# Linear attention and expert FFN in fp32 on one core: the last block's scores taken ahead of the preceding block's values, and a 22nd buffer of expert weights

## The chip, the cores and the metric

One Trainium2 chip, one core of it. The metric is the time on the device in microseconds (us), the median of three runs. All data is fp32.

## What is computed

The input `x` is (4, 128, 64, 64): four images, 128 channels, 4096 tokens each. Two layers follow each other.

```
x = x + conv_attention(group_norm(x))          # layer 0: softmax(e1^T e2) over 4096 x 4096 tokens
t = tokens(x)                                  # (4, 4096, 128)

# layer 1, attention with a scan: 8 heads, q_proj (8, 128), W_kv (2048, 128)
k, v = silu(layernorm(t) @ W_kv)               # per head 128 keys and 128 values
s = q_proj . k                                 # one score per token and head
m = cummax(s);  e = exp(s - m)
out = cumsum(e * v) / cumsum(e)                # along the tokens
t = t + mean over heads(out)

# layer 1, experts: 64 experts, each takes its 8 best tokens
p = softmax(layernorm(t) @ gate_w^T) over the tokens;   topv, topi = top_k(p^T, 8)
pooled = sum of the 8 tokens weighted by topv           # (4, 64, 128)
h = gelu(pooled @ weight1[e] + b1);  o = h @ weight2[e] + b2
t[topi] += o * topv
```

The cut leaves out the layer norm ahead of the gate's sum and the reshapes. The expert weights are 64 experts x 2 matrices of 128 x 512: 64 units of 512 KB, where a unit is one matrix of two experts.

## The kernel before

**Stages.** Layer 0 takes about the first 1460 us of the span. Attention with the scan runs in `loop()` (L1133) over `NB` = 32 blocks of 512 tokens, about 25 us each. Then come the gate's end and the pooling of the chosen tokens, the experts in 16 groups of four (`first`, `turn`, `second`, `gather`, L1362 to L1414), and the sums that go out.

**A block n of the loop.** `keys(n + 1)` makes the keys of the next block (L364, L365: TensorE, then a Silu on ScalarE for each of 8 heads). `weights(n)` turns the exponentials `es` (L902), copies them (L904), and builds `em` on GpSimd (L917). `weighted` multiplies `em` by the reciprocal sums `rb` (L926, VectorE). `values(n)` makes the values: eight matmuls `pv` of 128 x 512 (L938), each followed by a Silu on ScalarE (L942). `totals(n)` sums values per group of 64 tokens (L954), and VectorE adds these up in `before` (L964). `score(n + 1)` (L839) and `scan(n + 1)` follow, and `outputs(n)` (L974, L981) makes the result, which L986 adds to `t`.

**The scan.** `scan` is a chain over four engines: a copy of the scores in two halves (L851, VectorE), a running maximum (L856), the difference (L860), an Exp on ScalarE (L861), a copy into `es` on GpSimd (L866), and on VectorE a running sum (L871) and its reciprocal (L876). `spread` sends the reciprocals through DRAM so that they reach all partitions: `rd<-rr` (L884) and `rb<-rd` (L891), on the queue of SyncE.

**What sets the order.** TensorE's order is written out by hand (`manual_schedule`). A planner orders the other engines, by the data they wait for and by its estimates; the program then runs each engine's list as it stands. So the place of an Exp among the Silus of ScalarE, or of a copy among VectorE's products, is fixed when the program is built. The banks that `pk`, `pe`, `gtr`, `pv`, `pl` and `ltr` use are one pool of three (`l1kv`): a `pv` waits until the third tile before it has been read.

**The gate.** For each block, `gate_stats`, `gate_norm` (a Sqrt on ScalarE, L91, then `xg` at L96), `gate_turn` (L1023, L1025 into `xt2`) and `gate_logits` (L1031, L1035, and a maximum at L1038) run one or two blocks behind. `xg` and `xt2` are two tiles of 512 columns. ScalarE changes its function table at each change among Silu, Exp and Sqrt.

**The weights.** `load_units` (L1238) issues the 64 units on SyncE's queue, in the order in which they are used. There are `NW` = 21 places: 13 of the pool `fw`, 6 in `room` (which holds the keys and turned tokens during the loop), `wks` and `wvs` (the projections). All 21 are asked for right after the loop; each goes out once its place is free. After that `first` and `second` of each group ask for two more, which wait until the unit 21 places earlier has been used.

Of the kernel before, what the change touches and what calls it, by code (L numbers as in the profile page):

```python
# [8 lines left out]
F32 = mybir.dt.float32  # L9
# [4 lines left out]
P = 128  # L14
# [4 lines left out]
def conv_attn_hybrid_kernel(  # L19
# [23 lines left out]
    nc = tc.nc  # L43
    B, C, N = x.shape
# [6 lines left out]
    BLK = 512  # L51
    NBLK = N // BLK
    CPB = BLK // P
# [48 lines left out]
    wks = resid.tile([C, NH, C], F32, tag="wks", name="wks")  # L102
# [680 lines left out]
    GRP = BLK // H2  # L783
    EG = E // QG
    NB = B * NBLK
    NW = 21

    def layer1(pre, ready):

# [5 lines left out]
        with ExitStack() as kept, ExitStack() as l1:  # L795
# [39 lines left out]
            def score(n, ks):  # L835
                pss = ps_s.tile([P, BLK], F32, tag="s", name=f"{pre}ps_{n}")
                for h in range(NH):
                    g, r = h % QG, h // QG
                    nc.tensor.matmul(  # L839
                        pss[g * QW : (g + 1) * QW, :], qz[:, h, :], ks[h],  # L840
                        start=(r == 0), stop=(r == NR - 1),
                    )
                return pss
# [80 lines left out]
            def weighted(ems, rbs):  # L924
                for em, rb in zip(ems, rbs):
                    nc.vector.tensor_mul(em, em, rb.rearrange("p s h j -> p (s h) j"))  # L926
                return [em.rearrange("p (s h) j -> p s h j", s=2) for em in ems]
# [69 lines left out]
            rden = lgp.tile([P, B // 2], F32, tag="rden", name=f"{pre}rden")  # L997

            total = lgp.tile([P, C], F32, tag="total", name=f"{pre}total")
            gmv, grs, xgs, gate_xts, picks, eighth, cts, lefts = {}, {}, {}, {}, {}, {}, {}, {}  # L1000

            def gate_stats(n):
# [4 lines left out]
            def gate_norm(n, engine):  # L1007
                grs[n] = gp.tile([P, CPB], F32, tag="grs", name=f"{pre}grs_{n}", bufs=2)
                root = roots(grs[n], gmv[n])
                xgs[n] = gp.tile([P, CPB, C], F32, tag="xg", name=f"{pre}xg_{n}")  # L1010
                for c in range(CPB):
                    normalise(
                        engine, xgs[n][:, c, :], n * CPB + c, gmv[n][:, c, 0:1],
                        grs[n][:, c : c + 1],
                    )

                nc.gpsimd.tensor_copy(rs1[:, bass.ts(n, CPB)], grs[n])
                return root

            def gate_turn(n, ps):  # L1020
                ptr = ps.tile([P, CPB, P], F32, tag="kv", name=f"{pre}gtr_{n}")
                for c in range(CPB):
                    nc.tensor.transpose(ptr[:, c, :], xgs[n][:, c, :], ident)  # L1023
                gate_xts[n] = gp.tile([P, BLK], F32, tag="xt2", name=f"{pre}xt2_{n}")
                nc.scalar.copy(gate_xts[n], ptr.rearrange("p c x -> p (c x)"))  # L1025

            def gate_logits(n, ps):
# [105 lines left out]
            def loop():  # L1133
                if ready:
                    ks = keys(0, xt_of[0], range(NH // 2, NH), kss, ps_kv)
                else:
                    for n in range(2):
                        turned(n, tokens(n, xl_place), xt_of[n], ps_kv, pre)
                    keys(0, xt_of[0], range(NH), kss, ps_kv, pre)
                made = scan(0, score(0, kss))  # L1140
                rbs = spread(0, made[1])
                for n in range(NB):
                    more = n + 1 < NB
                    if more:
                        ks = keys(n + 1, xt_of[n + 1], range(NH // 2), kss, ps_kv, pre)
                    if n >= 1:
                        gate_stats(n - 1)
                    if not more:
                        gate_norm(n - 1, nc.vector)
                    if n + 2 < NB:  # L1150
                        xls = tokens(n + 2, xl_place)
                    if n == 0:

                        banks = [
                            ps.tile([P, 2, BLK], F32, tag=tag, name=f"{pre}pk_{tag}")[:, 0, :]
                            for ps, tag in ((ps_o, "o"), (ps_t, "t"))
                        ]
                        ks += keys(
                            n + 1, xt_of[n + 1], range(NH // 2, NH), kss, ps_kv, pre, banks
                        )  # L1160
                    es, rr, _ = made
                    ems = weights(n, es)
                    if n >= 2:
                        gate_turn(n - 2, ps_kv)
                    if more and n > 0:
                        ks += keys(n + 1, xt_of[n + 1], range(NH // 2, NH), kss, ps_kv, pre)
                    k0 = n - (B // 2 * NBLK + 2)
                    with ExitStack() as order:
                        if k0 == 0:
                            with tc.issue_after(made[2][1]):  # L1170
                                order.enter_context(tc.issue_after(select(0)))
                        if 0 <= k0 < NBLK:
                            left = gp.tile([P, BLK], F32, tag="left", name=f"{pre}left_0_{k0}")
                            marked = pick_mark(0, k0, left)
                            if marked is not None:
                                order.enter_context(tc.issue_after(marked))
                        if 1 <= k0 <= NBLK:
                            order.enter_context(tc.issue_after(pick_turn(0, k0 - 1, ps_kv)))
                        if k0 == NBLK:
                            divisors(0)  # L1180
                        aas = weighted(ems, rbs)
                    vs, last = values(n, xt_of[n])
                    if n >= 2:
                        best = gate_logits(n - 2, ps_kv)
                    if not more:
                        gate_turn(n - 1, ps_kv)
                    if 1 <= k0 <= NBLK:
                        pick_add(0, k0 - 1)
                    with tc.issue_after(last):
                        if n >= 1 and more:  # L1190
                            gate_norm(n - 1, nc.gpsimd)
                        if n == 0 and ready:
                            roots(rs1[:, bass.ts(B - 1, NCH)], mv1[:, bass.ts(B - 1, NCH), :])
                    if n + 2 < NB:
                        copied[n + 2] = turned(n + 2, xls, xt_of[n + 2], ps_kv, pre)
                    totals(n, vs)
                    if not more:
                        best()
                        best = gate_logits(n - 1, ps_kv)
                    if more:  # L1200
                        pss = score(n + 1, ks)
                        with ExitStack() as order:
                            if 0 <= k0 < NBLK:
                                with tc.issue_after(copied[n + 2]):
                                    exp = pick_exp(0, k0)
                                order.enter_context(tc.issue_after(exp))
                            made = scan(n + 1, pss)
                        rbs = spread(n + 1, made[1])
                        if 0 <= k0 < NBLK:
                            with tc.issue_after(made[2][1]):  # L1210
                                pick_keep(0, k0)
                    outputs(n, rr, aas, vs)
                    if n >= 2:
                        best()
# [3 lines left out]

            l1.close()
            pool = opener(l1, pre)  # L1220
            fwp = pool("fw", NW - 2 - ROOM)
            fo = pool("l2fo")
            fs = pool("l2fs", 2)
            ps_a = pool("l2a", 4, space=PSUM)
# [13 lines left out]
            def load_units(m):  # L1238
                for _ in range(m):
                    n = len(unit_weights)  # L1240
                    if n >= len(units):
                        return

                    if n % NW >= NW - 2:
                        w = wvs if n % NW == NW - 1 else wks.rearrange("d h e -> d (h e)")
                    elif n % NW >= NW - 2 - ROOM:
                        w = room[:, n % NW - (NW - 2 - ROOM), :]
                    else:
                        w = fwp.tile([P, FH + FC * C], F32, tag="fw", name=f"{pre}fw_{n}")
                    nc.sync.dma_start(out=w, in_=fw[units[n][0], units[n][1]])  # L1250
                    unit_weights[units[n]] = w
# [2 lines left out]
                w = unit_weights[layer, e // 2].rearrange("p (i x) -> p i x", i=2)[:, e % 2, :]  # L1254
                return w.rearrange("p (c o) -> p c o", c=FC) if layer else w

            load_units(NW)

            eos = fo.tile([P, B // 2, C], F32, tag="eo", name=f"{pre}eo")

# [29 lines left out]
            with tc.manual_schedule(engines={mybir.EngineType.PE}):  # L1290
# [25 lines left out]
                pool_tokens(0, total)  # L1316
                backs(2, nc.vector)
                best = gate_logits(NB - 1, ps_a)
                with tc.issue_after(copied[pre, NB - 1]):
                    backs(2, nc.scalar)  # L1320
                best()
# [233 lines left out]
```

## Time and profile before

| | us |
|---|---|
| median of 3 runs | 2386.18 (2384.77 to 2386.82) |
| the profiled execution | 2384.92 |
| its span | 2383.2 |
| what lies around the span | 1.7 |
| TensorE busy | 2340.1 (98%) |
| VectorE busy | 1494.8 (63%) |
| ScalarE busy | 1208.1 (51%) |
| GpSimd busy | 304.2 (13%) |

The stages around the change, in times of the timeline (us from the span's start):

| stretch | what |
|---|---|
| 2212.6 to 2237.0 | block 30: keys of 31, values of 30, scores of 31, outputs of 30 |
| 2237.0 to 2263.1 | block 31: scan of 31, values of 31, outputs of 31 |
| 2263.1 to 2289.9 | gate of the last block, choice of tokens, pooling |
| 2289.9 to 2353.2 | the 16 groups of experts |
| 2353.2 to 2383.2 | sums and output |

A busy TensorE is not a TensorE at its peak, since the ends of matmuls are modelled. In a line of the timeline the first number is the start, the second the time from the start of the first to the end of the last instruction of the group; the bracket tells how long the engine was idle ahead of it and what ended that. The page's chain of work that ended last is empty in this profile, so the path is read from the timelines and the waits.

### The profile page before, as it was taken

The numbers are of one execution on the slowest core, as the hardware profiler recorded it, in microseconds if no ns is written. First come the engines' busy times: TensorE is split into PE (matmuls) and PEld (weight loads), VectorE is DVE, ScalarE is ACT, GpSimd is POOL, SyncE is SP. The second block draws the span as 40 slices with busy tenths as digits, with TensorE's granted clock in tenths as the row PEclk, the third lists the DMA queues.
The fourth block names the chain that finished last, engine by engine and source line by source line (L and its number), as shares of the span: only waits on it lengthen the run. The fifth ranks groups of instructions, "written<-read, shape, count | busy, mean of one in ns | idle before, by whom it ended". The sixth has DMA issues, their size and how long they took to land.

```text
span 2383.2 us, 45629 instructions
## 1 busy us (share of the span) xinstructions
PE 2340.1 (98%) x19416; PEld 1554.0 (65%) x19416; DVE 1494.8 (63%) x2593; ACT 1208.1 (51%) x1639; POOL 304.2 (13%) x338
## 2 busy tenths in 40 slices
PE   7999999999999999999999999999999999999897
PEld 3567777677778677778777775555555555655554
DVE  6666666666656666655555556666666677776655
ACT  5444444444443444443443335666666666666541
POOL 0000000000000000000000002333343333333300
PEclk9999999999999999999999999999999999999999
DMA  3200110000100000020000000212112121112388
GB/s 83 75 23 19 41 39 1 17 13 23 49 25 1 23 7 23 18 52 1 1 1 1 1 1 19 55 38 55 38 38 55 38 54 39 38 38 55 118 307 322
DMA packets 61765, 109.93 MB, mean 46 GB/s; under 512 B 10096, under 2 KB 35184, under 8 KB 61552
## 3 DMA queue, kind: packets, MB, share of 16 engines
q1 hardware_dynamic: 57824, 101.22, 14.8%
q10 hardware_dynamic: 3728, 5.71, 0.7%
q8 instruction: 154, 2.52, 0.4%
q14 instruction: 59, 0.48, 0.1%
HBM read 85.40 MB, written 8.91 MB: 40 GB/s over the span
## 4 chain that ended last, share of the span: by engine, by line


## 5 line engine op out<-in xcount | busy, mean ns | idle before, releaser
L608 PE MATMUL av<-pr,am 64*128 64x512 f32 x4096 | 1057.2, 591 | 0.0
L587 ACT ACTIVATE pr<-sc 128x1024 f32<-128x1024 f32 x512 | 523.8, 1023 | 675.4 <-PE sc L583 606.7
L590 DVE TENSOR_TENSOR acc<-acc,pr 128x1024 f32<-128x1024 f32 x480 | 587.0, 1223 | 436.0 <-ACT pr L587 435.9
L608 PEld LDWEIGHTS av<-pr,am 64*128 64x128 f32 x4096 | 634.6, 187 | 260.4 <-issue 45.2
L583 PE MATMUL sc<-e,e 64*128 64x512 f32 x2048 | 618.9, 594 | 1.9 <-DMA e<-ee 1.9
L583 PEld LDWEIGHTS sc<-e,e 64*128 64x128 f32 x2048 | 317.3, 188 | 106.5 <-issue 19.5
L364 PE MATMUL pk<-room,wks 128*128 128x512 f32 x508 | 238.3, 607 | 2.0 <-ACT room L365 1.7
L938 PE MATMUL pv<-wvs,room 128*128 128x512 f32 x512 | 227.0, 596 | 2.5 <-ACT v L942 2.1
L942 ACT ACTIVATE v<-pv 128x512 f32<-128x512 f32 x256 | 152.7, 597 | 69.7 <-PE pv L938 69.7
L938 PEld LDWEIGHTS pv<-wvs,room 128*128 128x128 f32 x512 | 97.0, 191 | 121.9 <-issue 114.2
L926 DVE TENSOR_TENSOR em<-em,rb 128x1024 f32<-128x1024 f32 x64 | 78.4, 1224 | 154.4 <-DMA rb<-rd 154.4
L828 POOL MEMSET ew<- 128x1024 f32 x1 | 1.0, 952 | 1360.9 <-PE av L608 1360.9
L365 ACT ACTIVATE room<-pk 128x512 f32<-128x512 f32 x254 | 146.8, 597 | 54.4 <-PE pk L364 54.2
L364 PEld LDWEIGHTS pk<-room,wks 128*128 128x128 f32 x508 | 89.4, 189 | 107.6 <-issue 79.0
L917 POOL TENSOR_TENSOR em<-et,mask 128x1024 f32<-128x1024 f32 x64 | 122.6, 1937 | 79.0 <-ACT et L904 79.0
L96 POOL TENSOR_SCALAR xg<-t,gmv,grs 128x128 f32<-128x128 f32 x120 | 95.2, 806 | 287.3 <-DVE grs L92 209.4
L974 PEld LDWEIGHTS po<-v,em 64*64 64x64 f32 x4096 | 111.6, 133 | 29.1 <-DVE before L964 26.7
L974 PE MATMUL po<-v,em 64*64 64x128 f32 x4096 | 119.9, 271 | 1.9 <-issue 1.9
L876 DVE RECIPROCAL rr<-rr 128x512 f32<-128x512 f32 x32 | 107.3, 3353 | 1.1
L861 ACT ACT_TABLE_LOAD x24 | 30.8, 1283 | 121.1 <-DVE ss L860 121.1
L964 DVE TENSOR_TENSOR before<-before,pt 128x128 f32<-128x128 f32 x256 | 72.6, 284 | 9.6 <-PE pt L954 3.8
L871 DVE TENSOR_TENSOR_SCAN rr<-ones,state,ss 128x512 f32<-128x512 f32 x28 | 42.0, 1501 | 48.7 <-ACT ss L861 46.6
(203 smaller groups left out, 2031.5 us busy)
## 6 DMA issues: line engine op xcount, KB each, us to landing
rb<-rd SPq DMA_DIRECT2D x128, 256.0 KB
fw<-in_fw_dram SPq DMA_DIRECT2D x40, 512.0 KB
room<-in_fw_dram SPq DMA_DIRECT2D x18, 512.0 KB
t<-in_xtok_dram SPq DMA_DIRECT2D x32, 256.0 KB
e<-ee SPq DMA_DIRECT2D x63, 128.0 KB
x<-in_x_dram SPq DMA_DIRECT2D x12, 512.0 KB
e<-ee SPq DMA_DIRECT2D x63, 64.0 KB
out_dram<-t SPq DMA_DIRECT2D x8, 256.0 KB
```

Of the source, the lines that this page charges most:

```text
L96: i = engine.tensor_scalar(out=dst, in0=t[:, chunk, :], scalar1=mean, scalar2=rs, op0=ALU.subtract, op1=ALU.mult)
L364: nc.tensor.matmul(pk, wks[:, h, :], xt, start=True, stop=True)
L365: nc.scalar.activation(kss[h], pk, AF.Silu)
L583: nc.tensor.matmul(sc[:, u, :], e2[halves[u], p, :], e1[halves[u], :], start=True, stop=True)
L587: nc.scalar.activation(pr, sc, AF.Exp)
L590: added.append(nc.vector.tensor_add(acc, acc, pr).ins)
L608: nc.tensor.matmul(av, am[h, j, :], pr[h, u, :], start=(j == 0), stop=(j == NCH - 1))
L876: inverse = nc.vector.reciprocal(rr, rr).ins
L917: nc.gpsimd.tensor_tensor(em, eq.unsqueeze(2).to_broadcast([P, 2 * NH, H2]), mask.unsqueeze(1).to_broadcast([P, 2 * NH, H2]), ALU.mult,)
L938: nc.tensor.matmul(pv.rearrange("p h d -> p (h d)"), xt[:, bass.ts(2 * q + s, P)], wvs[:, bass.ts(m, BLK)], start=True, stop=True,)
L942: last = nc.scalar.activation(v[:, bass.ts(m, HPB), :], pv, AF.Silu).ins
L974: nc.tensor.matmul(po[s * H2 : (s + 1) * H2, u, q, :], aas[q][half, s, h, :], vs[2 * q + s][half, h, :], start=(q == 0 and h == 0), stop=F ...
```

## The change

For block 30 alone (`n + 2 == NB`), `score`, `scan` and `spread` of block 31 are written ahead of `values(30)` instead of after `totals(30)`. In block 31, `gate_norm(30)` is written after `weights(31)` and `gate_turn(29)` instead of ahead of them. `xg` and `xt2` become the halves of one tile, `gate_room`. That tile is the 22nd place for weights: 21 units are asked for after the loop as before, and the 22nd after the last `gate_logits`, whose matmul is the last reader of the tile. The pool `fw` stays at 13 buffers.

```diff
-    NW = 21
+    NW = 22
...
+            gate_room = gp.tile([P, 2 * BLK], F32, tag="gate_room", name=f"{pre}gate_room")
...
-                xgs[n] = gp.tile([P, CPB, C], F32, tag="xg", name=f"{pre}xg_{n}")
+                xgs[n] = gate_room[:, :BLK].rearrange("p (c d) -> p c d", c=CPB)
...
-                gate_xts[n] = gp.tile([P, BLK], F32, tag="xt2", name=f"{pre}xt2_{n}")
+                gate_xts[n] = gate_room[:, BLK:]
...
-                    if not more:
-                        gate_norm(n - 1, nc.vector)
...
                     if n >= 2:
                         gate_turn(n - 2, ps_kv)
+                    if not more:
+                        gate_norm(n - 1, nc.vector)
...
                         aas = weighted(ems, rbs)
+
+                    sooner = n + 2 == NB
+                    if sooner:
+                        rr_next = scan(n + 1, score(n + 1, ks))
+                        rbs_next = spread(n + 1, rr_next[1])
                     vs, last = values(n, xt_of[n])
...
-                    if more:
+                    if sooner:
+                        made, rbs = rr_next, rbs_next
+                    elif more:
                         pss = score(n + 1, ks)
...
-            fwp = pool("fw", NW - 2 - ROOM)
+            fwp = pool("fw", NW - 3 - ROOM)
...
-                    if n % NW >= NW - 2:
-                        w = wvs if n % NW == NW - 1 else wks.rearrange("d h e -> d (h e)")
-                    elif n % NW >= NW - 2 - ROOM:
-                        w = room[:, n % NW - (NW - 2 - ROOM), :]
+                    part = n % NW - (NW - 3 - ROOM)
+                    if part >= 0:
+                        w = (
+                            *(room[:, i, :] for i in range(ROOM)),
+                            wks.rearrange("d h e -> d (h e)"), wvs, gate_room,
+                        )[part]
...
-            load_units(NW)
+            load_units(NW - 1)
...
                 best = gate_logits(NB - 1, ps_a)
+                load_units(1)
```

## The prediction

> **What bounds the kernel now.** The page's chain is empty, so I read, in order: the waits of TensorE from 2205 to 2266 us, the timelines of the engines there, the windows of 2 us for clock and DMA, then the experts' timeline. TensorE stands still in block 31 alone:
>
> ```profile
> PE pe L902 <- POOL es L866: 2.6, 2, 1.8
> PE pv L938 <- ACT v L942: 2.1, 1, 2.1
> PE po L974 <- issue: 1.9, 1, 1.9
> ```
>
> The columns are total, times, longest. The first row is the wait for the scan of block 31, since no keys of a block 32 cover it. TensorE:
>
> ```profile
> 2235.93 1.09 PE L981 MATMUL po<-before,rr 128*64 128x128 f32 x16
> 2238.80 0.44 PE L902 MATMUL pe<-ident,es 128*128 128x128 f32 x2 [1.77 <-POOL es L866]
> ...
> 2240.78 5.29 PE L938 MATMUL pv<-wvs,room 128*128 128x512 f32 x8
> 2248.17 3.70 PE L938 MATMUL pv<-wvs,room 128*128 128x512 f32 x8 [2.10 <-ACT v L942]
> ```
>
> Eight rows are four `pv`, which take 3.43 us where nothing stops them (7.03 us for sixteen rows, pitch 0.857 us per `pv`). Here the fifth starts 7.39 us after the first: 3.96 us are lost to ScalarE, which changes tables for a Sqrt between the first and the second Silu. VectorE in block 30, then ScalarE:
>
> ```profile
> 2225.77 1.22 DVE L926 TENSOR_TENSOR em<-em,rb 128x1024 f32<-128x1024 f32 x1 [4.66 <-DMA rb<-rd]
> 2228.47 1.22 DVE L926 TENSOR_TENSOR em<-em,rb 128x1024 f32<-128x1024 f32 x1 [1.49 <-DMA rb<-rd]
> ```
>
> ```profile
> 2236.36 1.28 ACT L861 ACT_TABLE_LOAD   x1 [5.73 <-DVE ss L860]
> 2237.65 0.63 ACT L861 ACTIVATE ss<-ss 128x512 f32<-128x512 f32 x1
> ```
>
> `rb` of block 30 arrives at 2225.77 and 2228.47. The table load of the scan's Exp itself waits for the difference L860: ScalarE idles 5.73 us ahead of it although nothing else hinders a load. In the experts:
>
> ```profile
> 2343.90 1.04 PE L1397 MATMUL po<-room,hs 128*4 128x128 f32 x28 [0.80 <-DMA room<-in_fw_dram]
> ...
> 2349.03 0.28 PE L1397 MATMUL po<-wks,hs 128*4 128x128 f32 x2 [0.80 <-DMA wks<-in_fw_dram]
> ```
>
> Up to 2340 TensorE runs through. The last groups wait for weights: 2339.82 to 2344.88 to 2350.00, 5.1 us for four units, so 1.28 us per unit. The DMA share is about 1.0 from 2296 to 2348 and 0.00 from 2284 to 2290. So the experts end when the units do, counted from the first use of weights at 2289.87.
>
> **What the Trainium skill says.** "TensorE: Matmul & The Clock Gate", Part 1 (The HAM clock gate): after a window of 3.4 us with little work the clock drops to half until a busy window has passed. The trace agrees: after the gaps from 2237 to 2240 the clock reads 0.70 and 0.50 in the two windows from 2240 to 2244, and 0.73 and 0.50 from 2274 to 2278. The same part says that ScalarE and VectorE are strictly in order; the timelines agree. "ScalarE: Activation LUTs", What ACT_TABLE_LOAD costs and Terms, gives about 2.7 us for a load; the trace has 1.28 us, which I use. "DMA: Bandwidth & Descriptors", Issuing engines are not separate DMA queues: all transfers share the same 16 engines. The trace agrees in that the second `rb` pair came 7.09 us after issue in block 29, and 7.62 us in block 30 with one unit issued behind it.
>
> **The change, part by part.** The built program of the changed kernel gives each engine's order, and there the planner's choice decides. VectorE: first half of the score copy, `em` 0 of block 30, second half, maximum, difference, `em` 1, running sum, reciprocal, then the gate and `before`. ScalarE: three Silus of `values(30)`, Exp with its load, a load of Silu, five Silus.
>
> *Block 30, the new wait.* Keys of 31 end at 2220.65 as before, scores take 1.85 us (2230.43 to 2232.28), so the first `pv` starts at 2222.50. Silu follows 1.06 us behind, so the third ends at 2225.88. Then ScalarE holds Exp. On VectorE the second half of the copy sits behind `em` 0, which waits for `rb` until 2225.77: it starts at 2227.00. From there to the end of the difference is 2.26 us in the present scan (0.34 + 1.28 + 0.69 with overlaps): 2229.3. Load 1.28, Exp 0.63, load 1.28: the fourth Silu starts at 2232.6 and ends at 2233.2. TensorE has three banks, so it gets six `pv` done, to 2222.50 + 6 x 0.857 = 2227.65, and stands until 2233.25. Cost: +5.6 us. The Exp that waited in an idle ScalarE now stands ahead of five Silus, and TensorE is behind those.
>
> Two `pv` bring it to 2234.97; from there to the last of L981 are 9.51 us before (2227.51 to 2237.02) less the 1.85 of scores: 2242.63. VectorE is in time: running sum and reciprocal end at 2236.3, the gate's maximum about 2238.7, eight additions to `before` by 2241.2, L981 needs the last about 2242.
>
> *Block 31, what is saved.* `es` is ready by 2233.1 (Exp 2231.3, two copies 1.67), so the 2.6 us go. From 2242.4 the transposes take 0.9; `et`, `xt2`, load, first Silu, load, Sqrt (0.3), load follow: 2243.1, 2243.6, 2244.2, 2245.5, 2246.1, 2247.4, 2247.7, 2249.0. Sqrt's input is ready at 2246.8: `t` at 2243.4, `ew`, statistics, and one `em` that waits for GpSimd until 2245.3. The second Silu ends at 2249.6, and the fifth `pv` starts there against 2248.17 now: +1.4. That is 5.6 lost less 4.2 saved (11.15 us from the end of L981 to the fifth `pv` now, 7.0 after). `rb` of 31 comes 7.45 us after the reciprocal, 2243.8, earlier than needed. Moving `gate_norm` costs nothing: in the built order its Sqrt still follows the first Silu.
>
> *The clock.* 5.6 us without work hold a whole window of 3.4 us. The work that follows runs at half clock until a busy window is over, on average about 3.4 us of it: +1.7, between 0 and 3.4. In block 31 TensorE would again idle some 2.6 us ahead of the fifth `pv`; now it is 2.1 us at a clock that stays 1.00. I take 0, between 0 and 1.7.
>
> *The pause of 1.86 us in L974* has no semaphore behind it. Transfers of `room`, `wvs` and `fw` run at 387 GB/s just then, and do so after. I keep it; between -1.9 and 0.
>
> *Queues.* On SyncE four `room` units and `wks` now go out from 2223.3 instead of `wks` there and `room` at 2231.55. They share the engines with the second `rb` pair: one unit cost it 0.5, so 4 more about 2 us, to 2230.5. `em` 1 then ends at 2231.7 instead of before 2231.3: 0.4 us later for the running sum, which has room. I take 0, at most +1. GpSimd does `xg` of 29 after `es` (done 2241.0, needed 2242.9): 0. The joined gate tile has the same readers and writers: 0. Its cover is the idle part of GpSimd; without it, 3 us per block.
>
> *From 2263.1 to 2289.9* the orders of the engines are the same: shift only.
>
> *The 22nd unit* goes out after `fw`'s 13th (2273.7), lands in the stretch where DMA idles, and one unit less is left: -1.3 us (1.28 at the end; 1.4 from 43 units between 2290.9 and 2350). Cover: the last groups of experts have about 2 us of slack each (5.1 against some 3.0 of work), so TensorE can follow. If not, 0.
>
> *Sum.* +1.4 + 1.7 - 1.3 = +1.8 us on 2384.92: 2386.7 for a profiled execution. That execution lies 1.26 below the median of the runs, so the forecast is 2386.18 + 1.8 = 2388.0 us.
>
> **The rivals.** A measurement of this kernel can tell about 0.2%, 4.8 us, from no change.
>
> *The scan is hidden, as its place in the code suggests.* Then the 5.6 and the 1.7 don't arise: 2388.0 - 7.3 = 2380.7. For it: the banks and ScalarE have slack in most of block 30. Against it: the difference would have to be done before 2226, and `em` 0 stands ahead of it until 2227. Only an `rb` some 3 us earlier decides for this. Chance 0.08.
>
> *The half clock decides: slower.* Place: TensorE in the two `values`. Price: two windows in block 30 (3.4) and one in block 31 (1.7) give 1.4 + 5.1 - 1.3 = +5.2: 2391.4. Beyond 4.7 us lost, so 9.4 us at half clock, it is slower than 0.2%. For it: short idle already halves the clock at 2274. Against it: the gap of 2.1 us at 2246 and the one of 1.86 at 2257 don't. Chance 0.17.
>
> *The further unit buys nothing*, because the end is set by TensorE or by slots that come free at the same times: +1.3, so 2389.3. For it: TensorE runs without a gap to 2340. Against it: the waits for `room` and `wks` above. Chance 0.10.
>
> **How the numbers follow.** Forecast (stop moved from block 31 to block 30, unit pays) 0.65; rivals 0.08, 0.17, 0.10. Faster by over 0.2% (below 2381.4): the first rival, 0.08. Slower (above 2391.0): most of the second and a little of the rest, 0.17. Same: 0.75. The range 2383.5 to 2391.5 takes in each open cost by itself (pause gone: 2386.1; clock without effect: 2386.3; clock at its most in block 30: 2389.7), and leaves out the first rival and half of the second.
>
> **What would show it.** In the changed profile: TensorE idle about 5.6 us inside `pv` of block 30, released by ScalarE; ScalarE idle about 3.4 us ahead of the Exp's load, released by L860; VectorE's second half-copy right after `em` 0; a clock of 0.5 around 2234 to 2238; no wait of `pe` for `es`; a fifth `pv` of block 31 about 1.4 to 3.1 us later than 2248.2; and first weights used about 3 us later than 2289.9, yet an end of the experts only 1.8 later. I am wrong if TensorE waits less than 3 us in block 30, or if `rb` lands so late that block 31 waits for it.

## The result, and the profile after

| | before | after |
|---|---|---|
| median of 20 runs, us | 2386.11 (2382.90 to 2389.61) | 2389.26 (2386.39 to 2394.61) |
| profiled execution, us | 2384.92 | 2387.22 |
| its span, us | 2383.2 | 2385.4 |

The ratio is 1.0015, with a 95% interval of 1.0008 to 1.0022: some 3 us slower. The interval leaves out 1, so the loss is clear of noise, but it is under 0.2%. The forecast was 2388.0 us, its range 2383.5 to 2391.5.

The waits of TensorE from 2205 to 2270 us, after (columns as before: total, times, longest):

```profile
PE pv L938 <- ACT v L942: 9.0, 2, 5.7
PE po L974 <- issue: 0.9, 1, 0.9
PE otr L1287 <- DVE t L986: 0.8, 1, 0.8
```

The wait of `pe` for `es` (2.6 us before) is gone, and the wait of `pv` for ScalarE has grown from 2.1 to 9.0 us. The timeline of TensorE shows its two places, in `values(30)` and in `values(31)`:

```profile
2219.98 1.92 PE L839 MATMUL ps<-room,qz 128*32 128x512 f32 x16
2221.83 5.42 PE L938 MATMUL pv<-wvs,room 128*128 128x512 f32 x12
2232.91 3.78 PE L938 MATMUL pv<-wvs,room 128*128 128x512 f32 x4 [5.66 <-ACT v L942]
...
2244.72 0.66 PE L902 MATMUL pe<-ident,es 128*128 128x128 f32 x4
...
2245.65 3.93 PE L938 MATMUL pv<-wvs,room 128*128 128x512 f32 x8
2252.91 5.40 PE L938 MATMUL pv<-wvs,room 128*128 128x512 f32 x8 [3.34 <-ACT v L942]
```

Twelve rows, six `pv`, go through; then comes the stop of 5.66 us. Why, VectorE's timeline shows:

```profile
2222.12 0.43 DVE L851 COPY ss<-ps 128x256 f32<-128x256 f32 x1 [1.77 <-PE ps L839]
2225.32 1.23 DVE L926 TENSOR_TENSOR em<-em,rb 128x1024 f32<-128x1024 f32 x1 [2.78 <-DMA rb<-rd]
2226.46 0.42 DVE L851 COPY ss<-ps 128x256 f32<-128x256 f32 x1
...
2228.23 0.69 DVE L860 TENSOR_TENSOR ss<-ss,mm 128x512 f32<-128x512 f32 x1
```

The second half of the score copy stands behind the product `em`, and that waits 2.78 us for a DMA. So the difference L860 ends at 2228.9, and ScalarE, whose next instruction is the table load for the Exp, waits for it with five Silus behind:

```profile
2229.03 1.28 ACT L861 ACT_TABLE_LOAD   x1 [3.66 <-DVE ss L860]
2230.32 0.63 ACT L861 ACTIVATE ss<-ss 128x512 f32<-128x512 f32 x1
2230.97 1.28 ACT L942 ACT_TABLE_LOAD   x1
2232.26 1.58 ACT L942 ACTIVATE v<-pv 128x512 f32<-128x512 f32 x3
```

The work behind both stops runs slowly. The windows of 2 us (the third number from the end is the clock that TensorE was granted) show half clock in two places:

```profile
core 0: us, PE busy (x) PEld busy (x) DVE busy (x) ACT busy (x) POOL busy (x), PEclk, DMA share, GB/s
...
2234.00:2236.00 2.00, 2.00 (x4) 0.94 (x3) 2.00 (x1) 0.60 (x1) 0.00 (x0) 0.50 0.00 0
2236.00:2238.00 2.00, 2.00 (x35) 0.76 (x36) 0.06 (x1) 1.26 (x2) 0.00 (x0) 0.82 0.03 7
...
2254.00:2256.00 2.00, 2.00 (x4) 0.97 (x3) 0.00 (x0) 0.67 (x2) 0.00 (x0) 0.50 0.00 0
2256.00:2258.00 2.00, 2.00 (x4) 0.74 (x4) 0.00 (x0) 1.03 (x2) 0.00 (x0) 0.70 0.00 0
```

In the experts the last groups still wait for weights, now those of two `room` places:

```profile
2345.97 0.28 PE L1409 MATMUL po<-room,hs 128*4 128x128 f32 x2 [0.81 <-DMA room<-in_fw_dram]
...
2351.08 1.04 PE L1409 MATMUL po<-room,hs 128*4 128x128 f32 x28 [0.80 <-DMA room<-in_fw_dram]
```

**Where the time went.** The trace of after stands 0.67 us earlier than that of before when the keys of block 31 end (2219.98 against 2220.65), with the same work ahead; so I count from there. The traced execution of after is the third fastest of its 20 and lies 2.0 us below their median (that of before 1.2); its mean granted clock is 0.997, where 13 of the others have 0.995 or 0.994. What the stretches tell of the clock holds for these two executions.

| stretch | before | after | difference | predicted |
|---|---|---|---|---|
| end of keys of 31 to end of L981 in block 30 | 16.37 | 24.80 | +8.4 | +7.3 |
| to the fifth `pv` of block 31 | 11.15 | 8.13 | -3.0 | -4.2 |
| to the first use of weights | 41.70 | 41.17 | -0.5 | 0 |
| to the end of the last group of experts | 63.35 | 61.20 | -2.15 | -1.3 |
| to the end of the span | 29.98 | 30.12 | +0.1 | 0 |
| sum | | | +2.9 | +1.8 |

Over the whole spans the difference is +2.2, since after was 0.67 us ahead at the start of the count.

### The profile page after: what moved, and what is told of

It reads as the page before. It is cut to its first block, busy times and chain, and to the rows that moved or that the text cites. A ratio compares the mean times of both kernels' runs of the same rounds, so it can differ in the third digit from the quotient of the medians.

```text
span 2385.4 us, 45716 instructions
## 1 busy us (share of the span) xinstructions
PE 2337.9 (98%) x19416; PEld 1551.8 (65%) x19416; DVE 1496.5 (63%) x2593; ACT 1208.2 (51%) x1640; POOL 303.7 (13%) x338
## 5 line engine op out<-in xcount | busy, mean ns | idle before, releaser
L917 POOL TENSOR_TENSOR em<-et,mask 128x1024 f32<-128x1024 f32 x64 | 122.5, 1935 | 81.4 <-ACT et L904 81.4
L96 POOL TENSOR_SCALAR gate_room<-t,gmv,grs 128x128 f32<-128x128 f32 x120 | 94.8, 802 | 285.6 <-DVE grs L92 191.0
L974 PEld LDWEIGHTS po<-v,em 64*64 64x64 f32 x4096 | 111.9, 133 | 27.6 <-DVE before L964 25.1
L974 PE MATMUL po<-v,em 64*64 64x128 f32 x4096 | 120.2, 271 | 1.0 <-issue 0.9
```

Source lines behind the costliest of these rows:

```text
L96: i = engine.tensor_scalar(out=dst, in0=t[:, chunk, :], scalar1=mean, scalar2=rs, op0=ALU.subtract, op1=ALU.mult)
L917: nc.gpsimd.tensor_tensor(em, eq.unsqueeze(2).to_broadcast([P, 2 * NH, H2]), mask.unsqueeze(1).to_broadcast([P, 2 * NH, H2]), ALU.mult,)
L974: nc.tensor.matmul(po[s * H2 : (s + 1) * H2, u, q, :], aas[q][half, s, h, :], vs[2 * q + s][half, h, :], start=(q == 0 and h == 0), stop=F ...
```

## The experiments

Each was timed in five rounds beside runs of the kernel before. My theory is that of the prediction: the early scan costs a stop of TensorE and half clock behind it, and the unit gives back about 1.3 us. Rivals: the unit gives nothing, the scan is hidden, or the clock has nothing to do with the stops. The table has for each kernel the two stretches that matter (A from the end of the keys of 31 to the first weights, B from there to the end of the experts), and how much time the granted clock took away between 2220 and 2304 us (over the windows of 2 us, the sum of 2 us times what the clock lacks to 1). A, B and the clock are of one trace each.

| kernel | median, us | difference to before in its batch, us | ratio to before (95%) | A | B | clock |
|---|---|---|---|---|---|---|
| before | 2386.11 |  | | 69.22 | 63.35 | 5.10 |
| after | 2389.26 | +3.15 | 1.0015 (1.0008 to 1.0022) | 74.10 | 61.20 | 5.14 |
| scan_only | 2390.21 | +5.03 | 1.0022 (1.0013 to 1.0032) | 75.17 | 62.68 | 5.12 |
| unit_only_b | 2384.01 | -1.66 | 0.9990 (0.9982 to 0.9999) | 69.54 | 62.30 | 5.12 |
| warm | 2383.38 | -1.80 | 0.9992 (0.9984 to 1.0000) | 69.51 | 61.30 | 0 |
| exp_last | 2382.30 | -2.88 | 0.9989 (0.9982 to 0.9995) | 67.87 | 61.91 | 3.42 |
| scan_first | 2385.88 | +0.21 | 1.0001 (0.9992 to 1.0009) | 70.59 | 61.93 | 5.12 |
| exp_last_sqrt | 2380.38 | -5.29 | 0.9980 (0.9971 to 0.9989) | 66.39 | 61.75 | 3.42 |
| first_sqrt | 2381.00 | -4.67 | 0.9983 (0.9976 to 0.9989) | 68.20 | 60.69 | 3.42 |
| em_vector | 2387.58 | +2.89 | 1.0007 (0.9999 to 1.0015) | 73.41 | 62.34 | 6.84 |

The kernel before was run anew with each batch; its medians there were 2386.11 with after, 2385.18 with scan_only, unit_only, warm and exp_last, 2385.67 with unit_only_b, scan_first, exp_last_sqrt and first_sqrt, and 2384.69 with em_vector. They differ by up to 1.4 us, so I compare kernels of different batches by the third column.

**scan_only: the early scan without the unit.**

```diff
-    NW = 22
+    NW = 21
...
-            gate_room = gp.tile([P, 2 * BLK], F32, tag="gate_room", name=f"{pre}gate_room")
...
-            load_units(NW - 1)
+            load_units(NW)
...
-                load_units(1)
```

> The early scores, scan and spread of block 31 and the moved gate step alone, with 21 places for weights as before. Theory (the Exp of the scan stops ScalarE among the Silus of block 30, TensorE stands about 5.7 us and then runs at half clock; the further unit gives back 1.3 to 2.2 us): TensorE idle about 5.7 us in block 30 as in the changed kernel, and a time 1.3 to 2.2 us above the changed kernel, so about +4.5 to +5.5 us on before. Rival (the joined gate tile and the 22nd unit are what costs): no more than +1 us on before.

Measured: 2390.21 us, ratio 1.0022, 5.0 us above before as expected. TensorE stops for 5.22 us in block 30 and 3.34 in block 31; the first of them:

```profile
2233.03 3.78 PE L938 MATMUL pv<-wvs,room 128*128 128x512 f32 x4 [5.22 <-ACT v L942]
```

So the slow part is the scan, and the unit is worth what lies between this kernel and after: B is 62.68 against 61.20, 1.5 us, with no half clock in either. That the scan is hidden is refuted.

**unit_only: the tile and the unit without the scan, first try.**

```diff
                     if n >= 1:
                         gate_stats(n - 1)
+                    if not more:
+                        gate_norm(n - 1, nc.vector)
...
-                    sooner = n + 2 == NB
-                    if sooner:
-                        rr_next = scan(n + 1, score(n + 1, ks))
-                        rbs_next = spread(n + 1, rr_next[1])
```

> The joined gate tile and the 22nd unit of weights alone, scan at its old place. Theory: the orders in blocks 30 and 31 are those of before, and the experts end 1.3 to 2.2 us earlier after the first use of weights, so a time 1.3 to 2.2 us below before. Rival (the unit or the joined tile costs): at or above before.

Measured: 6259.41 us, ratio 2.6243 (2.6209 to 2.6277), from a profile with 103084 instructions instead of 45716. The code tells why: with one tile for both blocks, `gate_norm(30)` at its old place fills the half that `gate_turn(29)` has yet to read; the gate of block 29 is then made from block 30's tokens. The profile has 44160 matmuls instead of 19416, which fits a pass through the program's second branch, where everything is computed once more; that it went there is read from the code. It says nothing of the unit. It does say that the move of `gate_norm` belongs to the joined tile, not to the scan.

**unit_only_b: the same with `gate_norm` at its new place.**

```diff
-                    sooner = n + 2 == NB
-                    if sooner:
-                        rr_next = scan(n + 1, score(n + 1, ks))
-                        rbs_next = spread(n + 1, rr_next[1])
...
-                    if sooner:
-                        made, rbs = rr_next, rbs_next
-                    elif more:
+                    if more:
```

> The joined gate tile, gate_norm at its new place behind gate_turn(n - 2), and the 22nd unit; scores and scan of block 31 at the old place. My theory: no stop in block 30 and no half clock there; the unit shortens the experts as it does in the whole change (from first weights used to their end 63.35 us before, 61.20 after), but part of the 2.15 is the clock, so 1.3 to 2.2 us below the kernel before, ratio 0.9991 to 0.9995. Rival (the further unit buys nothing, the end is set by TensorE): within 0.5 us of the kernel before, and the stretch of the experts stays at 63 us.

Measured: 2384.01 us, ratio 0.9990, 1.7 us below the kernel before. The weights are first used at 2289.88, before at 2289.87, with the same half clock in the first group; the last gather follows at 2352.18 instead of 2353.22. So the unit alone gives 1.04 us in the experts, which begin at the same time. The rival that it buys nothing falls: the stretch fell to 62.3 us, where that rival had 63, though the interval of the time itself ends just below 1. It is the half of the change that pays.

**warm: idle matmuls in the two stops.** Six matmuls of 128 x 512 ahead of the seventh `pv` of block 30 and three ahead of the fifth of block 31, into a bank that nobody reads.

```diff
+            spare = {(NB - 2, 1, 1, 0): 6, (NB - 1, 1, 0, 0): 3}
...
+                            for _ in range(spare.get((n, q, s, m), 0)):
+                                nc.tensor.matmul(
+                                    idle.rearrange("p u i c -> p (u i c)")[:, :BLK], ident,
+                                    wvs[:, :BLK], start=True, stop=True,
+                                )
```

> The changed kernel with matmuls into a PSUM tile that nobody reads, six ahead of the seventh values matmul of block 30 and three ahead of the fifth of block 31, where TensorE stands still; the result does not depend on them. Theory (half the clock after the stop costs 2.1 us in block 30 and some 1.8 us in block 31): clock 1.00 in both blocks, and about 3.9 us below the changed kernel. Rival (the clock record costs nothing, ScalarE sets the pace): the same time as the changed kernel within 1 us.

Measured: 2383.38 us, some 5 us below the changed kernel, each taken against before of its own batch. TensorE of this kernel in block 30:

```profile
2226.66 5.31 PE L940 MATMUL idle<-wvs,ident 128*128 128x512 f32 x12
2232.03 1.98 PE L947 MATMUL pv<-wvs,room 128*128 128x512 f32 x4
```

The stop is as long as ever, but the two `pv` behind it take 1.98 us instead of 3.78, and the clock is 1.00 in every window from 2220 to 2304. That this half clock follows from the stops is shown. The gain is about 1 us larger than the 3.9 us expected. A is 4.6 us shorter: 1.8 and 1.7 are the two groups of `pv`, 0.3 is the stop (5.37 us from the sixth `pv` to the seventh), and the pause in L974 of block 31 (0.86 us) doesn't appear, which the expectation didn't have. The medians' 5 us and this trace's 4.6 agree within the noise.

**exp_last: the Exp behind the last Silu.** The scores stay early; the scan's Exp is held until the last Silu of block 30 has been issued.

```diff
-                        rr_next = scan(n + 1, score(n + 1, ks))
-                        rbs_next = spread(n + 1, rr_next[1])
+                        pss_next = score(n + 1, ks)
                     vs, last = values(n, xt_of[n])
+                    if sooner:
+                        with tc.issue_after(last):
+                            rr_next = scan(n + 1, pss_next)
+                        rbs_next = spread(n + 1, rr_next[1])
```

> The changed kernel with the Exp of the early scan behind the last Silu of block 30 instead of behind the third. Theory: no stop in the values of block 30, no half clock there, the scan still early enough for block 31; 6 to 8 us below the changed kernel, so about 2381 to 2383 us where before has 2386. Rival (the early scan costs by its transfers or by VectorE's chain, not by ScalarE's order): within 2 us of the changed kernel.

Measured: 2382.30 us, some 6 us below the changed kernel, as expected, and 0.11% below the kernel before. TensorE and ScalarE of this kernel:

```profile
2221.35 7.13 PE L938 MATMUL pv<-wvs,room 128*128 128x512 f32 x16
```

```profile
2229.14 1.28 ACT L861 ACT_TABLE_LOAD   x1
2230.43 0.63 ACT L861 ACTIVATE ss<-ss 128x512 f32<-128x512 f32 x1
```

All eight `pv` run through, and the load has no idle time ahead of it. VectorE's order up to the running sum is that of the changed kernel, `em` and the difference L860 included. So the stop came from the place of the Exp in ScalarE's list. A cost shows elsewhere: the reciprocal comes later, and L981 takes 2.91 us instead of 1.09 while it waits for `before`.

**scan_first: the difference ahead of the products.** Here VectorE does the scan up to L860 before the `em` of block 30, and the Exp keeps a place among the Silus. (`rr_next[2][2]` is the difference L860.)

```diff
-                        aas = weighted(ems, rbs)
+                        if n + 2 != NB:
+                            aas = weighted(ems, rbs)
...
                         rbs_next = spread(n + 1, rr_next[1])
+                        with tc.issue_after(rr_next[2][2]):
+                            aas = weighted(ems, rbs)
```

> As changed, but VectorE does both halves of the score copy, the maximum and the difference of block 31 ahead of em 0 and em 1 of block 30, so that the difference no longer stands behind the wait for rb; ScalarE has the Exp behind the second Silu. My theory (the late difference makes the stop): the difference ends near 2224.6, load, Exp and load follow to 2227.9, the third Silu ends at 2228.5, and TensorE stops some 2.4 us ahead of its sixth pv instead of 5.66 ahead of the seventh; a gap of this length left the clock at 1.00 elsewhere, so the 2.1 us at half clock go too: 5.4 us below the changed kernel, 2383.9 us. Block 31 keeps its idle 3.3 us. Rival (any Exp in the middle of the Silus costs the same, since it brings two table loads): a stop over 4 us and less than 2 us gained. Rival (em late, L974 waits for it): a wait for em in L974 that gives the gain back.

Measured: 2385.88 us, ratio 1.0001: some 3 us below the changed kernel, not the 5.4 expected. TensorE of this kernel:

```profile
2223.41 4.56 PE L938 MATMUL pv<-wvs,room 128*128 128x512 f32 x10
2230.48 2.84 PE L938 MATMUL pv<-wvs,room 128*128 128x512 f32 x6 [2.51 <-ACT v L942]
```

The stop is the 2.4 us that I had worked out (2.51), ahead of the sixth `pv`, and no half clock follows it. So the late difference makes 3.1 of the 5.66 us, and the table loads and the Exp among the Silus the rest. But the clock took away as much as in the changed kernel: it is half from 2276 to 2280 and from 2292 to 2298, where after has 1.00. What was saved at one stop was lost at later, short gaps. The mechanism (the late difference) held, my sum for the clock did not.

**exp_last_sqrt: also the Sqrt of block 31 behind its Silus.**

```diff
-                    if not more:
-                        gate_norm(n - 1, nc.vector)
...
                     if not more:
-                        gate_turn(n - 1, ps_kv)
+                        with tc.issue_after(last):
+                            gate_norm(n - 1, nc.vector)
...
                     if not more:
                         best()
-                        best = gate_logits(n - 1, ps_kv)
+                        gate_turn(n - 1, ps_kv)
...
                     outputs(n, rr, aas, vs)
+                    if not more:
+                        best = gate_logits(n - 1, ps_kv)
```

> As exp_last (Exp of block 31 behind the last Silu of block 30), and in block 31 gate_norm of 30 is written behind the last Silu, its transposes behind the totals and its logits behind the outputs, so that no Sqrt with its two table loads stands between the first and the second Silu. My theory: the idle of 2.4 us ahead of the fifth pv of block 31 goes, the Sqrt and its load lie behind the last Silu where ScalarE has 2 us to spare, and a later load of Sqrt falls away: 2.4 to 2.9 us below exp_last, 2379.6 us. Rival (the late gate of 30 becomes the next wait: its transposes wait for L96, or before for VectorE): a wait of 2 us or more ahead of L1025 or L981 and no gain. Rival (the units set the end, whatever comes before): the same time as exp_last, 2382.3.

Measured: 2380.38 us, ratio 0.9980 (0.9971 to 0.9989): some 8.4 us below the changed kernel and 5.3 below the kernel before. It has the lowest median of all, but its interval overlaps that of first_sqrt. TensorE in block 31 of this kernel:

```profile
2241.89 7.37 PE L938 MATMUL pv<-wvs,room 128*128 128x512 f32 x16
...
2252.31 1.01 PE L1025 MATMUL gtr<-ident,gate_room 128*128 128x128 f32 x4 [0.24 <-DVE gate_room L96]
```

No stop ahead of the fifth `pv`: eight take 7.2 us from the first start to the next group, in exp_last 9.9. The late gate costs 0.24 us at its transposes. Against exp_last 2.4 us are gained, each taken against before of its batch, where 2.4 to 2.9 were expected; the two traces differ by 1.6 us in A and B, since the pause in L974 is longer here (1.67 us against 0.85). The half clock that exp_last has from 2272.2 to 2275.6 lies now at that pause, from 2255.1 to 2258.5.

**first_sqrt: scan_first and the late Sqrt together.** Its edit is the sum of the two.

> scan_first and the late gate_norm of 30 in block 31 together. My theory: the two stops are of different causes and add up, so 5.4 us below the changed kernel for block 30 and 3.3 of idle plus 1.7 at half clock for block 31: some 9.5 to 10 us below the changed kernel, 2379.5 us, and below the kernel before by more than 0.2%. Rival (clock: with one stop gone, another gap later halves the clock as in the kernel before at 2274): 2382 us.

Measured: 2381.00 us, ratio 0.9983; some 7.8 us below the changed kernel. Both stops of `values` are treated, but the gain is 2 us short of the 9.5 to 10 expected: the time lies between that theory's 2379.5 us and the rival's 2382, and the half clock at other gaps, which the rival named, is there. Its stop in block 30 is again 2.51 us, as in scan_first; but here the half clock follows it:

```profile
2229.24 4.54 PE L938 MATMUL pv<-wvs,room 128*128 128x512 f32 x6 [2.51 <-ACT v L942]
```

Six rows take 4.54 us, in scan_first 2.84. The same gap cost 1.7 us more in one trace than in the other.

**em_vector: block 31's products by the mask on VectorE.**

```diff
-                    nc.gpsimd.tensor_tensor(
+                    engine = nc.vector if n == NB - 1 else nc.gpsimd
+                    engine.tensor_tensor(
```

> As changed, but in block 31 alone VectorE, not GpSimd, makes the two products em = et * mask (the operation of L917), so that GpSimd does no tensor operation while VectorE copies ew and gathers the statistics of the gate. My theory (the copies of ew and the first product with rb were held up by GpSimd's L917): the two copies take 0.85 us again instead of 1.99, no product takes over 1.25 us, the last statistics come about 3.1 us after the start of the copies instead of 5.0, the Sqrt no longer waits behind its table load, and TensorE idles 2.4 us ahead of the fifth pv of block 31 instead of 3.34; with the half clock behind that gap gone as well up to 2.7 us, without that 1.0 us below the changed kernel, 2386.6 to 2388.3 us. Rival (the slow copies come from the work's place in time, for instance from et arriving late or from the clock, not from GpSimd): the copies take 1.99 us as before, and the two further products of 1.22 us on VectorE make the Sqrt wait longer and the kernel slower than as changed.

Why this was tried: in the changed kernel the Sqrt of block 31 waits for the statistics, and VectorE is late with them. Its timeline there, then that of GpSimd, then ScalarE's Sqrt:

```profile
2245.64 1.99 DVE L909 COPY ew<-et 128x16 f32<-128x16 f32 x2
...
2248.53 2.00 DVE L926 TENSOR_TENSOR em<-em,rb 128x1024 f32<-128x1024 f32 x1
2250.45 0.17 DVE L88 BATCH_NORM_AGGREGATE gmv<-gst 128x2 f32<-128x6 f32 x1
```

```profile
2245.69 3.76 POOL L917 TENSOR_TENSOR em<-et,mask 128x1024 f32<-128x1024 f32 x2 [3.12 <-ACT et L904]
```

```profile
2250.66 0.30 ACT L91 ACTIVATE grs<-gmv,eps 128x4 f32<-128x4 f32 x1 [0.96 <-DVE gmv L88]
```

The last statistics (L88) stand behind the product. In the kernel before the two copies take 0.85 us and the product 1.22 to 1.23. With GpSimd out of the way, VectorE and ScalarE of em_vector:

```profile
2246.55 0.26 DVE L909 COPY ew<-et 128x16 f32<-128x16 f32 x2
...
2250.01 2.35 DVE L927 TENSOR_TENSOR em<-em,rb 128x1024 f32<-128x1024 f32 x2
```

```profile
2249.32 1.28 ACT L91 ACT_TABLE_LOAD   x1
2250.62 0.30 ACT L91 ACTIVATE grs<-gmv,eps 128x4 f32<-128x4 f32 x1
```

The copies take 0.26 us, the Sqrt follows its load at once, and TensorE idles 2.40 us instead of 3.34, as expected to the tenth; the clock behind that gap stays at 1.00. That the slow copies come from their place in time is refuted. A shorter time is not shown: the median, 2387.58, is in the expected range, but it lies 2.9 us above before of its own batch, where after lay 3.15 above, and the two intervals overlap. The profiled execution (span 2386.2) is no shorter either; the clock took away 6.84 us in it.

The slow copies alone do not make the Sqrt wait. In exp_last they take 1.99 us too, but there the last two statistics stand ahead of the product:

```profile
2243.18 0.29 DVE L88 BATCH_NORM_AGGREGATE gmv<-gst 128x2 f32<-128x6 f32 x2
2244.27 1.23 DVE L926 TENSOR_TENSOR em<-em,rb 128x1024 f32<-128x1024 f32 x1 [0.79 <-POOL em L917]
```

Its Sqrt follows the load at once, and TensorE idles 2.39 us. So in these runs it takes both: GpSimd in the way, and a product ahead of the last statistics in VectorE's list.

## Why the prediction was right

**The mechanism was.** The stop inside `pv` of block 30 was predicted at 5.6 us behind an Exp that waits for L860 behind `em` 0, and is 5.66. scan_only puts the loss in the scan, exp_last shows that it is the Exp's place, scan_first that the late difference makes 3.1 us of the stop. The waits for `es` are gone, and no DMA for `rb` of 31 holds anything up. (The second `rb` of block 30 was put at 2230.5; its product starts at 2228.84 without a wait, so the delay in the queue did not come.) Sum predicted +1.8, found +2.9 in the two traces, counted from the keys, and +3.15 in the medians. Two of the signs named beforehand were missed: the fifth `pv` of block 31 came 4.7 us later than before, not 1.4 to 3.1, and the first weights 4.2 us later, not 3.

**Block 30's clock, +1.7 predicted:** the two `pv` behind the stop lost 1.8 us (3.78 against 1.98 in warm). Two smaller terms were not in the sum: L974 takes 4.25 us instead of 3.72, and the stop begins 0.3 us later, counted from the keys. With these block 30 costs 8.4 instead of 7.3 us.

**Block 31, the step that was mis-sized:** "Sqrt's input is ready at 2246.8", hence a fifth `pv` 7.0 us after the end of L981, and "I take 0, between 0 and 1.7" for the clock. The fifth came after 8.1 us, and the clock cost the 1.7 (5.40 us for eight rows against 3.70). I had taken VectorE's times from the kernel before, where GpSimd's L917 was nearly over when the copies began; the earlier scan lets L917 begin together with the copies, and both they and the product ahead of the last statistics are held up. em_vector, without L917, idles 0.94 us less, and no half clock follows there. A border of the clock's windows cuts that gap into 0.84 and 1.56 us. Whether the half clock's absence is due to the shorter gap or to this cut, one trace doesn't tell (see the last section).

**What was kept as it was, and changed:** the pause in L974 fell from 1.86 to 0.86 us, and the half clock of the kernel before at 2274 does not appear after: from the end of L981 in block 31 to the first weights it is 25.5 us instead of 26.7. "Shift only" held for the orders of the engines, not for their clock. The gap of 1.84 us ahead of that place (L1098 before, L1100 after) is in both traces. That these -2.2 us cancelled most of block 31's surplus (1.2 us of waiting and 1.7 of half clock) is luck, not foresight, and so is part of the forecast's nearness.

**The unit, -1.3 predicted:** 1.04 us in unit_only_b, 1.5 between scan_only and after. The kernel before has half clock from 2292 to 2296, in the first group of experts, and after has none there. The rest of the 2.15 is that: scan_only, without the unit and without half clock there, has B 0.67 us shorter than before.

**The rivals.** The hidden scan and the unit that buys nothing are refuted by runs. The rival of the half clock is half true: its price in block 31 came, its second window in block 30 lay inside the stop.

**What stays open:** what the pause named "issue" in L974 is. It is 0.85 to 2.34 us in block 31 of nine kernels and absent there in warm; no run took it apart. Nor is it known why L974 of block 30 takes 4.25 us.

## What to carry to other kernels

Work that is moved ahead brings all its instructions into the in-order lists of every engine: ask for each what stands behind it, and put one that waits (here an Exp with its table load) behind those on which the busiest engine depends. The same early scan cost some 6 us more with its Exp ahead of five Silus than behind them. When a change moves work of a few us, read its effect from a stretch that begins at the same work in both traces, and count the windows of half clock apart, before a cause is named.

## What the runs showed of the hardware

**Half clock comes in portions.** Over 2220 to 2304 us the time that the clock took away was 0, 3.42, 5.10 to 5.14 or 6.84 us in ten kernels: 0, 2, 3 or 4 times 1.71, so portions of 3.42 us at half clock. They don't belong to a place. A gap of 2.51 us led to one in first_sqrt and not in scan_first, one of 3.34 us did in the changed kernel and one of 2.40 in em_vector didn't, and gaps of 1.8 us at 2274 did in some. The Trainium skill, "TensorE: Matmul & The Clock Gate", Part 1 (The HAM clock gate), says that the activity window runs freely, so that the same kernel meets it in another phase; the traces agree. The page gives the window as 3413 ns.

The traces show more. Read at steps of 0.1 us, they let the ends of each stretch of half clock be placed. In each of the nine traces that have half clock from 2220 to 2304 us, all these ends lie on one grid of 3.41 us, and where the grid lies differs between the traces. (A window, below, is one step of this grid.) In the kernel before the starts are 2240.79, 2274.93 and 2292.00, which are 10 and 5 times 3.41 apart. On this grid the gap of 2.51 us lies inside one window in first_sqrt (2225.92 to 2229.33), and half clock begins at that window's end; in scan_first a border at 2228.65 cuts it into 0.68 and 1.83 us. The gap of 1.84 us lies, but for 0.03 us, inside one window in the kernel before (2271.52 to 2274.93) and is cut at 2277.66 in after. Among the gaps in `values`, windows at full clock with 2.1 us of idle time or more were followed by half clock, those with 1.94 or less were not. Idle time is not the whole of it, though: among small matmuls a window with 1.84 us idle was followed by half clock in scan_first (from 2273.02) and not in first_sqrt (from 2270.29). So the place of a gap on the grid matters; that it alone decides is not shown, and no run set it.

**VectorE and GpSimd shut each other out.** The Trainium skill, "SBUF — State Buffer", Who interferes with whom, says that a VectorE copy in a two-port mode, or an operation of it with two inputs in SBUF, shares ports with GpSimd, and that the later one waits until the other has ended. The traces agree: beside L917 (1.88 us each) the two small copies took 1.99 us, without it 0.26; the product begun at 2248.53 ended 1.08 us after L917 did and took 2.00, where it takes 1.22 by itself. The 0.85 us of the kernel before fit a shorter hold-up: its L917 runs from 2240.82 to 2244.58, its copies from 2243.85 to 2244.70.
